# Layer 1's first chunk gets its keys and queries inside layer 0's last batch

## The chip, the cores and the metric

The kernel runs on one core of one Trainium2 chip. A core has a matrix engine (TensorE, "PE" in the profile, with its weight loads as "PEld"), a vector engine (VectorE, "DVE"), a scalar engine for activations (ScalarE, "ACT"), a general engine (GpSimd, "POOL") and an engine that here only issues DMA transfers (SyncE, "SP"). Each engine takes its own instructions strictly in order and waits at semaphores for the others. The metric is the device time of one execution in microseconds; the profile shows one execution in detail.

## The reference

The input is `x`, 4 batches of 32 images of 128x128 pixels. Two layers follow each other.

Layer 0 is a Fourier attention block. Cut to its steps:

```python
xn = inorm(x)                                   # one channel per image
k, q, v = fno(xn, K), fno(xn, Q), fno(xn, V)    # 32 heads; spectral weights + a skip factor
p = softmax(q k^T over the 32 images of a batch)
av = p v
a = inorm(fno(av, P) + x)
m = fno(inorm(a), m0, inner_norm=True, act=gelu)
m = fno(m, m1, inner_norm=True)
out0 = inorm(m) + a
```

Layer 1 reads `out0` as 4 sequences of 4096 rows of 128 channels (an image's columns are the rows of the sequence). It normalises the rows, attends with additive scores (`score = sum_a w2[a] tanh(f_i[a] + g_j[a] + b1[a])`, strictly causal, exponentiated and normalised), adds, normalises again, and applies a router with 8 experts of which the best two are mixed, with a residual.

## The kernel before

**Layer 0** (`layer0`) loops over four batches `b`. A batch's spectrum `xd` was written to DRAM in the batch before. The stages of a batch: attention weights (`attention_weights`: products `pa` and `pb` of spectra on DVE and POOL, L473 and L475, summed by PE into `sp`, then a softmax from `mx` on, L509); the value products (L702 to L732: `xb` loaded from `xd` by SP in pairs, copied to PSUM by ACT as `xw`, multiplied with the weights `gb` into `u` on DVE, L719, and POOL, L717, summed over heads by PE into `po`); the back transform (`py`, evacuated into `yf`); a first spectrum, gelu (L844 to L854), a second spectrum (`spectra(1, gl)`: PE's `pz` and `px`, ACT's `z` and squares, DVE's `spec` and `part`, POOL's sum of the two, L804); and the last inverse transform into `xr`, stored to `x1` in DRAM by SP in four pieces (L910). For b below 3 the first stages of the next batch are put between these. The weights of layer 0 (`mcw`, `energy`, `cross`) are prepared once, before the first batch, ahead of `attention_weights(0, front)` in the program.

**Layer 1** (`layer1`) works on chunks of 1024 rows, four to a sequence. For a chunk, `prepare` loads `xc`, normalises it into `kx` (`norm_pieces`: statistics, aggregates, `scale` with a power on POOL, `apply`), transposes it into `xt` (`transpose_half`, PE's `pt`) and makes keys and queries (`as_keys`, `as_queries`: PE's `pz`, ACT's exponential, SP's DMAs that exchange halves of partitions into `kf` and `qf`). Keys of a sequence, `ke` and `kf`, stay in SBUF for its four chunks. The attention itself runs over units of up to 512 queries by 128 keys: PE makes `d` and `n` (L1297), ACT takes a logarithm and an exponential (L1350, L1362), DVE multiplies (L1355), POOL adds (L1358, L1359), ACT takes an exponential (L1366), and PE sums with `kx` (L1316). `finish` does the router and the experts.

**Order.** Outside of the attention's loop a scheduler of the framework orders each engine's instructions by priority (program order) and readiness by its own estimates. The attention's loop is under `manual_schedule`: its order is written out, and the remaining steps of other chunks (`pieces`) are dealt out among the units with budgets for DVE and POOL. Chunk 1's transposes are the first such pieces and stand on PE directly behind the first unit's `d`. Memory comes from pools; a pool entered after another has been left takes over its memory and waits for what still uses it. Before, all pools of layer 1 open after all of layer 0's are closed, and chunks 0 and 1 are prepared at the head of layer 1:

```python
    norm, pieces = begin(0, beside=False)
    norm_1, todo = begin(1, beside=False)
    for piece in norm + pieces + norm_1:
        piece[-1]()
```

The router and expert weights (`wr`, `we`, L936 to L984) and the maps `mq`, `mk` for queries and keys (L989 to L1014) are made ahead of that, all through one PSUM buffer (`misc`).

Of the kernel before, what the change touches and what calls it, by code (L numbers as in the profile page):

```python
# [7 lines left out]
F32 = mybir.dt.float32  # L8
AF = mybir.ActivationFunctionType
ALU = mybir.AluOpType  # L10
AX = mybir.AxisListType
PSUM = bass.MemoryType.PSUM

P = 128
B, T, H, C = 4, 32, 128, 128
# [5 lines left out]
A = 16  # L21
GROUP_SIZES = (6, 5, 5)
DSCALE = 128.0
NE = 8
IC = 1024
NB = IC // P
# [5 lines left out]
B1, W2, RB = 11, 27, 43  # L32
NSMALL = 51
# [41 lines left out]
NM = KX * KY  # L75
# [29 lines left out]
def layer0(  # L105
    tc, x, kq_modes, kq_mirror, vcw, pcw, m0cw, m1cw, mcol0, heads, heads_row, small_row, by_p, inv_cols, dram, x1
):
    nc = tc.nc
    pools = [tc.tile_pool(name="l0_const", bufs=1), tc.tile_pool(name="l0_ps", bufs=2, space=PSUM)]
    pools.append(tc.tile_pool(name="l0_x", bufs=2))  # L110
    const, ps, images = (p.__enter__() for p in pools)
# [21 lines left out]
    def columns(n):  # L133
# [8 lines left out]
    par = const.tile([P, NSMALL], F32, name="par")  # L142
    nc.sync.dma_start(out=par, in_=small_row.partition_broadcast(P))
    ident = const.tile([P, P], F32, name="ident")
# [14 lines left out]
    gb = const.tile([P, 2, 2, NM], F32, name="gb")  # L159
# [7 lines left out]
        tc.tile_pool(name="l0_modes", bufs=1),  # L167
    ]
    grp, small, modes = (p.__enter__() for p in work)
# [409 lines left out]


# [44 lines left out]
    prep_pool.__exit__(None, None, None)  # L625
    work = [tc.tile_pool(name="l0_big", bufs=1), tc.tile_pool(name="l0_xb", bufs=4)]
    big, late = (p.__enter__() for p in work)
    pools += work
    weights = attention_weights(0, front)

    for b in range(B):
# [63 lines left out]
        for x0 in range(0, KX, NK):  # L695
# [36 lines left out]
            nc.scalar.copy(rs[:, x0 : x0 + nk].rearrange("p x y -> p (x y)"), po)  # L732
        yf = big.tile([P, T, 2, KY], F32, name=f"yf_{b}", tag="spec")
# [126 lines left out]
        if b + 1 < B:  # L860
            normed = image_sums(b + 1, loaded)

# [53 lines left out]
def layer1(tc, x1, w1t_in, signs, vec17, expert_w, expert_b, router_w, small_row, out):  # L916
    nc = tc.nc
    nblk = T
    pools = [
        tc.tile_pool(name="l1_const", bufs=1),  # L920
        tc.tile_pool(name="l1_keys", bufs=2),
        tc.tile_pool(name="l1_work", bufs=2),
        tc.tile_pool(name="l1_small", bufs=2),
        tc.tile_pool(name="l1_ps", bufs=1, space=PSUM),
    ]
    const, keys, work, small, ps = (p.__enter__() for p in pools)

    tc.keep_in_program_order(nc.scalar.preload_act_table_set("natural_log_exp_and_others"))
    ident = const.tile([P, P], F32, name="ident1")
    make_identity(nc, ident)  # L930
    par = const.tile([P, NSMALL], F32, name="par1")
    nc.sync.dma_start(out=par, in_=small_row.partition_broadcast(P))
    nhalf = const.tile([P, 1], F32, name="nhalf1")
    nc.vector.memset(nhalf, -0.5)
    wr = const.tile([P, NE], F32, name="wr")
    nc.sync.dma_start(out=wr, in_=router_w)  # L936
    we = const.tile([P, NE, C], F32, name="we")
    nc.scalar.dma_start(out=we, in_=expert_w.rearrange("e d c -> d e c"))

    later = const.tile([P, 2, P], F32, name="later")  # L940
    nc.gpsimd.memset(later, 1.0)
    nc.gpsimd.affine_select(
        out=later,
        in_=later,
        compare_op=ALU.is_gt,
        fill=0.0,
        base=0,
        pattern=[[0, 2], [1, P]],
        channel_multiplier=-1,
    )  # L950

    rank = const.tile([P, NE], F32, name="rank")
    for e in range(NE):
        nc.vector.memset(rank[:, e : e + 1], float(NE - e))

    centre = const.tile([P, P + 1], F32, name="centre")
    nc.vector.tensor_scalar(centre[:, :P], ident, 1.0 / C, None, ALU.subtract)
    nc.vector.memset(centre[:, P:], 1.0 / C)

    banks = ["m"]  # L960

    def misc(name):
        banks.append(banks.pop(0))
        return ps.tile([P, 512], F32, name=name, tag=banks[-1])

    mean = const.tile([P, P], F32, name="mean")
    nc.vector.memset(mean, 1.0 / C)
    eb = work.tile([P, NE, C], F32, name="eb", tag="xt", bufs=1)  # L970
    nc.scalar.dma_start(
        out=eb.rearrange("p e c -> p (e c)"),
        in_=expert_b.rearrange("e c -> (e c)").partition_broadcast(P),
    )
    for w, row in (
        (wr, par[:, RB : RB + NE]),
        (we[:, :4].rearrange("p e c -> p (e c)"), eb[:, :4].rearrange("p e c -> p (e c)")),
        (we[:, 4:].rearrange("p e c -> p (e c)"), eb[:, 4:].rearrange("p e c -> p (e c)")),
    ):
        n = w.shape[1]  # L980
        pm = misc("pm")[:, :n]
        nc.tensor.matmul(pm, mean, w, start=True, stop=True)
        nc.vector.tensor_tensor(w, w, pm, ALU.subtract)
        nc.vector.scalar_tensor_tensor(w, row, 1.0 / C, w, ALU.mult, ALU.add)  # L984

    sg = const.tile([A + 1, P], F32, name="sg")
    nc.sync.dma_start(out=sg, in_=signs)  # L989
    w1t = const.tile([A, 2, P], F32, name="w1t")  # L990
    nc.sync.dma_start(out=w1t, in_=w1t_in)
    v17 = const.tile([A + 1, 2], F32, name="v17")
    nc.sync.dma_start(out=v17, in_=vec17)
    mq, mk = (const.tile([P, P], F32, name=n) for n in ("mq", "mk"))
# [6 lines left out]
    sgv = const.tile([P, 2], F32, name="sgv")  # L1001
    nc.vector.tensor_copy(sgv, pv[:, :2])

    one = const.tile([P, 1], F32, name="one1")
# [4 lines left out]
    off = const.tile([P, 2], F32, name="off")  # L1009
# [3 lines left out]
    kmul = const.tile([P, 1], F32, name="kmul")  # L1013
# [10 lines left out]
    def norm_pieces(src, dst, nb, beside=True):  # L1024


        st = small.tile([P, NB, 6], F32, name="st", tag="ln_st", bufs=3)
        mv = small.tile([P, NB, 2], F32, name="mv", tag="ln_mv", bufs=3)
        r = small.tile([P, NB], F32, name="r", tag="ln_r", bufs=3)
        mr = small.tile([P, NB], F32, name="mr", tag="ln_mr", bufs=3)  # L1030
# [37 lines left out]
    def prepare(b, i0, own, beside):  # L1068
# [4 lines left out]
        xc = work.tile([P, NB, C], F32, name="xc", tag="xc", bufs=4)  # L1073
        nc.sync.dma_start(out=xc, in_=x1[b, i0 : i0 + NB].rearrange("t w c -> w t c"))
        own_kx = kx[:, i0 : i0 + NB]
        xt = work.tile([P, IC], F32, name="xt", tag="xt", bufs=1)
        qe, qf = (work.tile([P, IC], F32, name=n, tag=n, bufs=3) for n in ("qe", "qf"))

        def as_keys(h):
# [4 lines left out]
            ks = work.tile([P, 512], F32, name="ks", tag="ks", bufs=1)  # L1084
# [19 lines left out]
        return (qe, qf), load + sums + after, pieces  # L1104

# [113 lines left out]
    chunks = [(b, i0) for b in range(B) for i0 in range(0, nblk, NB)]  # L1219
# [10 lines left out]
    state = {}  # L1230
    sums = {}
    live = {}

    def begin(c, beside=True):
        b, i0 = chunks[c]
        if i0 == 0:

            own = (keys.tile([P, nblk, C], F32, name=f"kx_{b}", tag="kx"),) + tuple(
                keys.tile([P, nblk * P], F32, name=f"{n}_{b}", tag=n) for n in ("ke", "kf")
            )  # L1240
        else:
            own = state[c - 1][0]
        qs, norm, pieces = prepare(b, i0, own, beside)
        state[c] = (own, qs)
        return norm, pieces

# [88 lines left out]
    norm, pieces = begin(0, beside=False)  # L1335
    norm_1, todo = begin(1, beside=False)
    for piece in norm + pieces + norm_1:
        piece[-1]()
# [79 lines left out]
    for p in reversed(pools):  # L1418
        p.__exit__(None, None, None)
# [72 lines left out]
```

## Time and profile before

| | |
|---|---|
| median of 3 runs | 3216.72 us (3215.26 to 3219.33) |
| the profiled execution's own time | 3214.14 us |
| its span, first to last instruction | 3212.4 us |
| mean granted TensorE clock | 0.963 |
| busy, share of span | PE 92%, DVE 72%, ACT 72%, POOL 66% |
| layer 0 | up to about 1095 us |
| layer 1 | from there to the end |

A row of the profile's timelines has start and duration in us, then engine, source line, operation, output<-inputs by the program's names, and in brackets how long the engine had idled and what ended that. Rows of neighbouring instructions of one kind are merged (x8). The table of stretches has, for each stretch, its length, each engine's busy time with the number of instructions, the granted clock as a share of full speed, the mean share of the 16 DMA engines, and GB/s. The line numbers are those of the kernel before.

### The profile page before, as it was taken

To read this page: it belongs to the slowest core of one execution; us is meant where nothing else is said; L and a number is where in the kernel's file an instruction comes from. 1 tells how busy PE (TensorE), PEld (TensorE's weight loads), DVE (VectorE), ACT (ScalarE), POOL (GpSimd) and SP (SyncE) were. 2 spreads that over 40 slices of the span, in tenths; PEclk is the share of its full clock that TensorE was granted. 3 is DMA by queue.
4 is the path that set the end of the run, shared out by engine and by line. 5 is a ranking of instruction groups with operands and counts; after the bars stand their busy time and mean duration, and the time that the engine had idled before them with its cause. 6 is when DMAs were issued, how large, how long until landed. Compare 5 with 4: busy or idle time off the path is not lost.

```text
span 3212.4 us, 53393 instructions
## 1 busy us (share of the span) xinstructions
PE 2971.1 (92%) x19698; PEld 1558.3 (49%) x19698; DVE 2317.7 (72%) x5072; ACT 2323.7 (72%) x3205; POOL 2134.2 (66%) x1879
## 2 busy tenths in 40 slices
PE   7899899899898699999999999999999999999997
PEld 5378367458558544444344443444444434444443
DVE  5767767768777556777666868866777777687887
ACT  2344344354344389999999999998999999999992
POOL 1631641461460278878788897889878889888773
PEclk7899899999998799999999999999999999999998
DMA  6301310230130111010110000011100010101000
GB/s 137 102 25 24 100 50 3 63 108 1 39 107 1 55 45 30 7 31 8 30 37 24 14 24 14 8 32 30 29 24 14 14 37 24 37 1 31 14 14 14
DMA packets 151925, 112.57 MB, mean 35 GB/s; under 512 B 36750, under 2 KB 140273, under 8 KB 151057
## 3 DMA queue, kind: packets, MB, share of 16 engines
q1 hardware_dynamic: 135825, 103.40, 12.0%
q10 hardware_dynamic: 15840, 5.77, 0.8%
q8 instruction: 156, 2.56, 0.3%
q14 instruction: 104, 0.85, 0.1%
HBM read 68.16 MB, written 20.00 MB: 27 GB/s over the span
## 4 chain that ended last, share of the span: by engine, by line
PE 59%; POOL 11%; ACT 8%; DVE 7%; issue 5%; DMA 0%; POOLq 0%; DVEq 0%; ACTq 0%; SPq 0%
PE d L1297 19%; PE po L1316 11%; PE px L1185 6%; ACT r L1350 4%; PE n L1297 4%; PE po L722 3%; POOL e L1359 3%; POOL e L1358 3%; PE four L257 2%; PE pv L252 2%; PE px L243 2%; PE px L242 2%; POOL kx L1050 1%; ACT e L1366 1%; PE pz L233 1%
## 5 line engine op out<-in xcount | busy, mean ns | idle before, releaser
L1355 DVE TENSOR_TENSOR r<-n,r 128x1024 f32<-128x1024 f32 (+1 forms) x1056 | 962.1, 953 | 479.9 <-PE n L1297 392.5
L1358 POOL TENSOR_TENSOR e<-r 128x512 f32<-128x512 f32 x528 | 673.0, 1275 | 268.7 <-DVE r L1355 268.1
L1350 ACT ACTIVATE r<-d 128x1024 f32<-128x1024 f32 (+1 forms) x1056 | 792.9, 802 | 65.5 <-PE n L1297 58.8
L1362 ACT ACTIVATE r<-r 128x1536 f32<-128x1536 f32 x528 | 783.5, 1484 | 16.7
L1359 POOL TENSOR_TENSOR e<-e,r 128x512 f32<-128x512 f32 x528 | 671.2, 1271 | 41.4
L1297 PE MATMUL d<-qe,ke 32*128 32x512 f32 (+3 forms) x2304 | 610.0, 604 | 38.3 <-ACT r L1350 36.5
L1316 PE MATMUL po<-e,kx 128*128 128x512 f32 (+3 forms) x1152 | 594.7, 605 | 15.0 <-POOL e L1371 15.0
L1297 PE MATMUL n<-qe,ke 32*128 32x512 f32 (+3 forms) x2304 | 607.4, 603 | 0.0
L1297 PE MATMUL d<-qf,kf 32*128 32x512 f32 (+3 forms) x2304 | 554.8, 556 | 0.0
L1297 PE MATMUL n<-qf,kf 32*128 32x512 f32 (+3 forms) x2304 | 554.5, 556 | 0.0
L1189 DVE SCALAR_TENSOR_TENSOR xc<-px,wgt,xc 128x128 f32<-128x128 f32 x1024 | 358.3, 350 | 41.2 <-PE px L1185 10.4
L1366 ACT ACTIVATE e<-e 128x512 f32<-128x512 f32 x528 | 325.6, 617 | 65.1 <-POOL e L1359 64.3
L1316 PEld LDWEIGHTS po<-e,kx 128*128 128x128 f32 x1152 | 175.6, 188 | 393.5 <-issue 310.1
L1297 PEld LDWEIGHTS d<-qe,ke 32*128 32x128 f32 x2304 | 177.4, 184 | 359.7 <-ACT r L1350 340.3
L717 POOL TENSOR_TENSOR u<-xb,gb 128x858 f32<-128x858 f32 (+1 forms) x120 | 234.8, 1987 | 115.1 <-PE po L722 104.7
L1297 PEld LDWEIGHTS d<-qf,kf 32*128 32x128 f32 x2304 | 221.5, 187 | 177.1 <-issue 164.7
L804 POOL TENSOR_TENSOR spec<-spec,part 128x264 f32<-128x264 f32 x64 | 55.0, 860 | 377.2 <-DVE part L801 173.6
L1185 PE MATMUL px<-we,x2t 128*128 128x512 f32 x512 | 265.2, 603 | 6.9 <-DVE xc L1189 6.0
L719 DVE TENSOR_TENSOR u<-xw,gb 128x858 f32<-128x858 f32 (+1 forms) x200 | 206.5, 1083 | 48.5 <-PE po L722 32.4
L1297 PEld LDWEIGHTS n<-qf,kf 32*128 32x128 f32 x2304 | 228.9, 186 | 19.8 <-issue 12.5
L722 PE MATMUL po<-u,pr 128*32 128x429 f32 (+1 forms) x1280 | 187.7, 537 | 18.3 <-POOL u L717 8.7
L1297 PEld LDWEIGHTS n<-qe,ke 32*128 32x128 f32 x2304 | 177.8, 183 | 10.0 <-DVE r L1355 1.2
(353 smaller groups left out, 4185.9 us busy)
## 6 DMA issues: line engine op xcount, KB each, us to landing
xb<-xd SPq DMA_DIRECT2D x128, 214.5 KB
xc<-x SPq DMA_DIRECT2D x31, 512.0 KB
x<-x SPq DMA_DIRECT2D x16, 512.0 KB
qf<-qe SPq DMA_DIRECT2D x64, 128.0 KB
out<-xc SPq DMA_DIRECT2D x15, 512.0 KB
xb<-xd SPq DMA_DIRECT2D x32, 198.0 KB
gb<-gd SPq DMA_DIRECT2D x4, 1056.0 KB
x<-in_x SPq DMA_DIRECT2D x8, 512.0 KB
```

What stands on the lines that cost most here:

```text
L717: nc.gpsimd.tensor_tensor(u, xb, gk, ALU.mult)
L722: nc.tensor.matmul(po[32 * j : 32 * j + 32], pr[:, i, k], u[:, r], start=i == 0 and k == 0, stop=i == 3 and k == 1,)
L1185: nc.tensor.matmul(px, x2t[:, k * P : (k + 1) * P], we[:, e0 : e0 + 4], start=True, stop=True)
L1189: nc.vector.scalar_tensor_tensor(xc[:, k], px[:, e], wgt[:, k, e0 + e : e0 + e + 1], xc[:, k], ALU.mult, ALU.add)
L1297: nc.tensor.matmul(o, k, q, start=turn == 0 or g > 0, stop=turn == 1 or g > 0)
L1316: nc.tensor.matmul(sums[c, h][:, q0 : q0 + c1 - c0], kx[:, jb], e[:, c0:c1], start=jb == 0, stop=is_last and q0 > 2 * P, skip_group_check= ...
L1350: nc.scalar.activation(r[:, g], d, AF.Ln, scale=1.0 / DSCALE)
L1355: nc.vector.tensor_tensor(r[:, g], part, r[:, g], ALU.mult)
L1358: nc.gpsimd.tensor_tensor(e, r[:, 1], r[:, 2], ALU.add)
L1359: nc.gpsimd.tensor_tensor(e, e, r[:, 0], ALU.add)
L1362: nc.scalar.activation(r, r, AF.Exp, scale=-1.0)
L1366: nc.scalar.activation(e, e, AF.Exp)
```

## The change

Layer 1 becomes a generator that is run in two parts. Its first part, entered from layer 0's last batch just behind the gelu in program order, opens a pool `l1_first` and prepares chunk 0 up to its keys and queries. That pool lies in SBUF at the other side of the memory, where layer 0's value weights `gb`, its spectra `xx` and the `xb` buffers were; these three now have pools of their own at that side, and are left in the last batch as soon as its value products are done. Chunk 0's input, its transposes and the scaled keys `ks` go through `spare`, a buffer of layer 0's images, and its PSUM through layer 0's `wide` buffers. The second part is the rest of layer 1. The constants that chunk 0 needs (`ident`, `sg`, `w1t`, `mq`, `mk`, the biases) move with it. In layer 0 `attention_weights(0, front)` moves ahead of the preparation of `mcw`, `energy` and `cross`. The cores of the diff:

```diff
 def layer0(..., dram, x1, first):
+    right = [
+        tc.tile_pool(name="l0_gb", bufs=1, side="right"),
+        tc.tile_pool(name="l0_modes", bufs=1, side="right"),
+    ]
...
+    prep_pool.__exit__(None, None, None)
+    pools.append(tc.tile_pool(name="l0_big", bufs=1))
+    right.append(tc.tile_pool(name="l0_xb", bufs=4, side="right"))
+    big, late = (p.__enter__() for p in (pools[-1], right[-1]))
+    weights = attention_weights(0, front)
     mcw, energy, cross = [], [], []
...
-    prep_pool.__exit__(None, None, None)
-    work = [tc.tile_pool(name="l0_big", bufs=1), tc.tile_pool(name="l0_xb", bufs=4)]
-    big, late = (p.__enter__() for p in work)
-    pools += work
-    weights = attention_weights(0, front)
...
             nc.scalar.copy(rs[:, x0 : x0 + nk].rearrange("p x y -> p (x y)"), po)
+        if b + 1 == B:
+            for p in reversed(right):
+                p.__exit__(None, None, None)
...
         logarithms()
         if b + 1 < B:
             normed = image_sums(b + 1, loaded)
+        else:
+            first((ps, images))
...
 def layer1(tc, x1, ..., out):
+    before, images = yield
+    first_pool = tc.tile_pool(name="l1_first", bufs=1, side="right")
+    first = first_pool.__enter__()
+    spare = images.tile([P, T, C], F32, name="spare", tag="x")
...
     def misc(name):
+        if not pools:
+            return before.tile([P, 512], F32, name=name, tag="wide")
...
+        if pools:
+            xc = work.tile([P, NB, C], F32, name="xc", tag="xc", bufs=4)
+            xt = work.tile([P, IC], F32, name="xt", tag="xt", bufs=1)
+        else:
+            xc, xt = spare[:, :NB], spare[:, NB : 2 * NB].rearrange("p k c -> p (k c)")
...
+    norm, pieces = begin(0, beside=False)
+    for piece in norm + pieces:
+        piece[-1]()
+    yield
+    pools += [ ... the pools of the rest of layer 1 ... ]
...
-    norm, pieces = begin(0, beside=False)
     norm_1, todo = begin(1, beside=False)
-    for piece in norm + pieces + norm_1:
+    for piece in norm_1:
         piece[-1]()
...
+        second = layer1(tc, x1, ..., out)
+        next(second)
         layer0(tc, ..., dram, x1, second.send)
+        for _ in second:
+            pass
```

Keys of the sequences 0 and 2 and queries of every third chunk live in `l1_first`, the others in the later pools, so that as many buffers rotate as before.

## The prediction

> **What bounds the kernel now.** I read the page first (busy shares and the chain of waits), then the table of stretches to find where layer 0 ends and layer 1 begins, then the timelines of those places.
>
> ```profile
> PE 59%; POOL 11%; ACT 8%; DVE 7%; issue 5%; DMA 0%; POOLq 0%; DVEq 0%; ACTq 0%; SPq 0%
> ```
>
> TensorE carries most of the chain, so work that is added to PE in a full stage costs its whole length, and a stage in which PE waits is where time can be won. The table of stretches (PE, PEld, DVE, ACT, POOL busy; granted clock; DMA share; GB/s):
>
> ```profile
> 1032.00:1041.00 9.00, 9.00 (x50) 9.00 (x50) 5.52 (x21) 4.26 (x10) 0.00 (x0) 0.58 0.01 2
> 1041.00:1063.00 22.00, 20.88 (x179) 20.17 (x177) 10.81 (x35) 9.03 (x22) 5.19 (x7) 1.00 0.00 1
> ...
> 1094.00:1126.00 32.00, 15.68 (x30) 6.81 (x30) 16.55 (x85) 1.37 (x2) 5.84 (x7) 0.50 0.38 107
> 1126.00:1134.00 8.00, 8.00 (x11) 2.17 (x10) 0.00 (x0) 2.40 (x3) 1.56 (x1) 0.50 0.42 96
> ```
>
> From 1094.9 us (the last result of layer 0) to about 1135 PE only prepares layer 1, half idle and at half clock. 1032 to 1063 is the last batch's second spectrum, where PE is full. The timeline of the passage:
>
> ```profile
> 1099.61 0.57 PE L982 MATMUL pm<-wr,mean 128*128 128x8 f32 x2 [5.84 <-DMA wr<-in_router_w]
> ...
> 1106.20 0.79 PE L997 MATMUL pm<-sg,w1t 16*128 16x128 f32 x2 [0.78 <-DVE we L983]
> ...
> 1119.51 1.65 POOL L1044 TENSOR_TENSOR r<-r,nhalf 128x8 f32<-128x8 f32 x1 [5.91 <-DVE r L1043]
> ...
> 1121.60 2.69 DVE L1050 TENSOR_SCALAR kx<-xc,r,mr 128x128 f32<-128x128 f32 x8
> ...
> 1132.73 1.02 ACT L1350 ACTIVATE r<-d 128x1024 f32<-128x1024 f32 x1 [1.35 <-PE d L1297]
> ...
> 1134.29 1.11 PE L1065 MATMUL pt<-ident,kx 128*128 128x128 f32 x4
> ```
>
> Line by line: PE's first step waits for the router weights until 1099.6; then come the expert weights, then the key and query maps and chunk 0's keys and queries; the power at 1119.5 and the `kx` at 1121.6 are chunk 1's norm; the attention's first logarithm is at 1132.7; chunk 1's transposes, which the hand-written order puts behind the first unit, end at 1135.4. From there the rows are attention proper. A second place is batch 0's attention weights, on DVE:
>
> ```profile
> 82.23 0.29 DVE L591 COPY mcw<-mcw_raw 128x66 f32<-128x66 f32 x1 [2.54 <-DMA mcw_raw<-in_m1cw]
> 82.44 1.21 DVE L473 TENSOR_TENSOR pb<-xp,xm 128x1024 f32<-128x1024 f32 x1
> 83.58 0.85 DVE L594 TENSOR_TENSOR msq<-mcw 128x66 f32<-128x66 f32 x1
> ...
> 89.52 1.21 DVE L473 TENSOR_TENSOR pb<-xp,xm 128x1024 f32<-128x1024 f32 x1
> ```
>
> DVE stands 2.54 us for the weights of the last convolution in the middle of its products `pa`, `pb`.
>
> **The change, part by part.** The order of each engine's instructions in the changed kernel can be read before it runs; the durations are those of the profiled execution (3214.14 us, of which 3212.4 are span).
>
> *A, weights of layer 0 later.* All of `mcw1`'s DVE work now stands after the last `pa` and before `mx`. From 79.7 (end of the `pa` before) to 89.52 DVE did four products (4 x 1.14 = 4.6 us) in 9.8 us: 5.2 us were the wait and the small operations. After 89.52 products follow without a gap to 102.05, so DVE sets the end there; POOL's `pb` (two of 1.9 us per three of DVE's groups of 4.5 us) and PE have room. The small operations, 2.6 us, now lie where DVE idled 5.28 us before `mx` (102.05 to 107.33), and their DMAs were issued by 82.2. The value products' first `xb` was issued at 83.4 and the DMA share has fallen to 0.23 from 96 on, so the value products can follow earlier. Gain 5.2; if the `xb` loads behind image 1's took half of it back, 2.6.
>
> *B, chunk 0's load.* It is put on SP's queue behind the last store of batch 2 and ahead of fifteen of the last batch's twenty pairs of `xb` loads. It overwrites the buffer which those stores read, so SP stands until the last has landed:
>
> ```profile
> 891.88 3.10 DMA x<-x
> ```
> ```profile
> 895.41 1.22 SPq L702 DMA_DIRECT2D xb<-xd  x2
> ```
>
> The first is of the chain of waits, the second of SP's timeline: landed at 894.98, next `xb` at 895.41 anyway. The wait costs 0.4 us. Behind it are the `xb` loads, ACT's copies `xw` and all of `u`. The load itself: a store of the same 512 KB moved at 291 GB/s in the DMA row, 1.8 us. The Trainium skill (DMA: Bandwidth & Descriptors, "Queues, rings and completion order") says that one queue's descriptors are consumed in ring order on each engine; so the `xb` start behind all of it: 2.2 us late by the rule. In the trace the DMA engines are only about half busy there (share 0.49 from 885 to 900), and the next use of `xb`, at 899.17, waited for DVE and not for DMA; the one at 903.32 waited 1.1 us for DMA while PE went on. I take 1.2, between 0 (a gain is excluded, as nothing is taken off the queue) and 3.7 (two late pairs).
>
> *C, chunk 0's norm, 955 to 968.* On DVE 8 statistics (1.7), 8 aggregates (0.6), scale with POOL's power (1.65) and one `kx`: from 957.7, when POOL's last `u` frees the memory, to 962.8. DVE was idle 6.98 us up to 963.28, its next evacuation of `yf`. So it is free, with 0.5 us to spare; the other seven `kx` (0.26 each) lie between evacuations 4 us apart. If the cover failed it would cost what it overruns, PE's `py` standing behind it. SP's three small loads and POOL's `ident` fall into idle time.
>
> *D, keys and queries of chunk 0, 1023 to 1053.* The two `pm` fall into the gelu stretch, in which PE idled 4.6 us: free. The rest goes to PE where it was full. `pv` and two `pc`: 1.4 us at half clock (the rows at 1108 to 1110). Eight transposes: two halves of 1.1 at half clock, 1.1 together at full. Four `pz`: 1.12 each at full clock (the rows of chunk 1), 2.08 at half. Then waits: two PSUM buffers for four `pz`, so the third `pz` waits for ACT's first exponential, the fourth for the second; and ACT now takes `z` only after its table load. Laid out by hand from the last gelu (1043.0): table 1.28, `z` 0.6, `ke` 0.69, DVE's `z` to 1046.0, `z` 0.38, `qe` 0.69, last `pz` to 1048.2, then the remaining 3.4 us of `px`: 1051.7 where it was 1044.7. Cost 7.3 (I allow 0.3 for late `ks` on POOL, 1.6 each, ahead of the `spec` sums). PE's work alone is 1.4 + 1.1 + 4.5 = 7.0; the ends are 5.5 (the chain's wait for ACT and DVE at 1051, 1.5 us, swallows a part) and 10.8 (all `pz` at half clock). The ten 128 KB DMAs that this issues on SP go when no other DMA runs and 30 us before the stores queued behind them.
>
> *E, the passage.* Gone: 1106.2 to 1132. Now PE issues two `d`, then `pm<-wr` (still 1099.6, for the router weights), `d`, `pm`, `d`, `pm`: at half clock, 2.07 each, to 1108.4. DVE does chunk 1's statistics between, the second `we` at 1108.5 to 1110, aggregates to 1111.8, POOL's power to 1113.7, four `kx` to 1115.2. PE stands there: chunk 1's transposes are next in its order. They end at 1116.3 where they ended at 1135.4: 19.1 us earlier. What is late next is chunk 1's norm, not chunk 0's keys. But PE has idled 7 us before it. The second unit's products (1135.4 to 1139.1) lose nothing by that, as they ran cold before too; the third's (2.2 us) ran at full clock:
>
> ```profile
> 1134.00:1136.00 2.00, 2.00 (x11) 1.31 (x14) 0.56 (x1) 1.57 (x2) 0.00 (x0) 0.50 0.47 108
> 1136.00:1139.00 3.00, 3.00 (x25) 2.12 (x18) 0.13 (x1) 0.51 (x1) 0.00 (x0) 0.57 0.00 0
> ```
>
> The Trainium skill's rule (TensorE: Matmul & The Clock Gate, "Part 1: The HAM clock gate") is that the clock is half by default and doubles after one busy window of about 3.4 us: then it is full by the third unit, 5 us after 1115.2, and nothing is lost. In this trace PE was full from 1031.6, after an idle of 4.6 us, and stayed at 0.50 until 1039.6, 8 us; by that the third unit runs cold and ends 2.0 us later. I take the trace: gain 19.1 - 2.0 = 17.1, by the rule 19.1. Bounds: 20.9 (clock full for the second unit already) and 14.4 (the fourth unit cold too, 2.7 more beyond ACT's pace of 4.1 us a unit). Behind it ACT's chain sets the pace as before.
>
> Sum: -5.2 + 1.2 + 0 + 7.3 - 17.1 = -13.8, to 3200.3 for the profiled execution. The median of the runs is 2.6 above that execution, so the forecast is 3216.7 - 13.8 = 3202.9. Ends: -5.2 - 20.9 + 5.5 = -20.6, and -2.6 - 14.4 + 10.8 + 3.7 = -2.5.
>
> **Rivals.** About 0.2%, 6.4 us, is what a measurement of this kernel can tell from no change.
>
> 1. The wait only moves. If chunk 1's norm does not come earlier (its first four `kx` ended at 1122.9), its transposes end at 1124, the gain in E is 11.4, or 9.4 with a cold third unit, and the sum is -6.1: 3210.6, at the edge of no change. For it: chunk 1's statistics share DVE with the `we` updates. Against it: its load no longer stands behind chunk 0's, and DVE loses half its work there.
>
> 2. Slower: the clock. The second spectrum runs at 1.00 with PE busy 20.88 us. If the waits in D drop the clock at 1043 and it stays down, that is up to 20.9 us more: sum +7.1, 3223.8. It decides from 13.8 of those 20.9 on. For it: an idle of 4.6 us before 1031.6 cost 8 us at 0.50. Against it: the waits in D are of 1 us.
>
> 3. More is won: PE warm at the second unit, D at its lower end, nothing lost in B: -20.6, 3196.1.
>
> That the change doesn't do what it says is excluded by the order: chunk 0's matmuls do stand in the last batch.
>
> **How the numbers follow.** My forecast 0.71, rival 1 0.15, rival 2 0.05, rival 3 0.09. The range 3196 to 3214 holds the forecast's ends and rival 1. Faster: 0.67 of the forecast, 0.06 of rival 1, 0.09: 0.82. Same: 0.04 and 0.09: 0.13. Slower: 0.05.
>
> **What would show it.** A: no wait at `mcw`, `mx` near 102. B: `xw` waits for DMA near 900. C: the `yf` evacuation where it was. D: from `py` to the last store 7 us longer, with `pz` waiting for ACT `ke` and `qe`. E: from the last `x` of layer 0 to the first long logarithm 26 us less, to chunk 1's transposes 19. I am wrong if D exceeds 12, if the clock at the second spectrum is not 1.00, or if the attention proper gets longer.

## The result, and the profile after

The changed kernel takes 3203.94 us (median of 4 runs, 3198.89 to 3207.05), beside 3215.99 us of the kernel before on the same chip (4 runs): a ratio of 0.996, 95% interval 0.9943 to 0.9978, or 12.05 us less. A second group of runs of the same changed kernel (after_again below) gave 10.8 us less. The profiled execution took 3203.55 us, of which 3201.8 are span, at a mean granted clock of 0.966. The chain of waits:

```profile
PE 55%; POOL 13%; ACT 9%; DVE 7%; issue 6%; DMA 1%; POOLq 0%; DVEq 0%; ACTq 0%; SPq 0%
```

TensorE still carries it. The table of stretches of the changed kernel (PE, PEld, DVE, ACT, POOL busy; granted clock; DMA share; GB/s) for the last batch and the passage:

```profile
1027.00:1036.00 9.00, 8.98 (x40) 8.64 (x41) 4.58 (x20) 4.07 (x10) 0.00 (x0) 0.50 0.01 2
1036.00:1044.00 8.00, 8.00 (x34) 5.71 (x34) 5.05 (x20) 5.82 (x10) 1.70 (x2) 0.78 0.07 16
1044.00:1066.00 22.00, 20.85 (x177) 20.15 (x176) 8.62 (x23) 6.53 (x17) 6.73 (x8) 1.00 0.24 55
1066.00:1078.00 12.00, 9.64 (x50) 9.67 (x51) 7.42 (x18) 1.53 (x4) 1.68 (x1) 0.57 0.01 1
...
1101.00:1124.00 23.00, 12.39 (x22) 4.27 (x26) 8.89 (x48) 3.10 (x3) 2.08 (x2) 0.50 0.35 107
```

PE is full from 1036 to 1044, where chunk 0's keys and queries were put in. The second spectrum (1044 to 1066) runs at full clock, as before, so the clock did not fall over the waits. The stretch behind it, the last inverse transform, is now at 0.57. The passage into layer 1 (1101 to 1124) is still half idle and at half clock, but shorter. PE's timeline of the passage:

```profile
1101.88 2.08 PE L1336 MATMUL d<-qe,ke 32*128 32x512 f32 x4 [1.31 <-DVE x L914]
...
1107.85 0.57 PE L1159 MATMUL pm<-wr,mean 128*128 128x8 f32 x2 [3.90 <-DMA wr<-in_router_w]
...
1114.35 2.08 PE L1159 MATMUL pm<-we,mean 128*128 128x512 f32 x2
...
1122.27 1.24 PE L1029 MATMUL pt<-ident,kx 128*128 128x128 f32 x4 [5.84 <-DVE kx L1014]
```

and ACT's:

```profile
1110.45 1.02 ACT L1388 ACTIVATE r<-d 128x1024 f32<-128x1024 f32 x1 [11.63 <-PE d L1336]
```

Attention products `d` now stand directly behind the last result of layer 0. Chunk 1's transposes wait 5.84 us for its norm: that is what is late next, as foreseen.

To compare stages between runs, each is measured between two events of its own profile (one profile for each kernel, us). *Value stage*: from the issue of the DMA `prd<-ph`, at the end of batch 3's attention weights, to the end of the first spectrum's `px`. *Gelu and second spectrum*: from the first `pv` behind that to the last `px`. *Last inverse*: to the end of the last `four`. *Passage*: to chunk 1's transposes. *Attention*: to the end of the span.

| kernel | value stage | gelu and second spectrum | last inverse | passage | attention |
|---|---|---|---|---|---|
| before | 129.24 | 51.82 | 31.52 | 40.52 | 2078.11 |
| before_with_a | 130.52 | 48.19 | 33.23 | 42.04 | 2079.24 |
| after | 130.45 | 56.84 | 35.40 | 21.71 | 2079.53 |
| after_again | 127.50 | 59.56 | 37.63 | 22.03 | 2079.63 |
| after_without_a | 130.32 | 58.35 | 34.40 | 21.43 | 2079.04 |
| keys_gap | 128.78 | 60.76 | 32.92 | 21.31 | 2079.47 |
| keys_gap2 | 131.64 | 53.49 | 31.17 | 21.73 | 2078.31 |
| norm1 | 128.83 | 66.80 | 43.62 | 16.25 | 2076.61 |
| norm1_lw | 128.87 | 62.82 | 43.62 | 5.03 | 2079.00 |
| gap2_lw | 131.74 | 56.32 | 31.13 | 17.13 | 2079.19 |
| all2 | 134.69 | 49.73 | 44.17 | 5.02 | 2079.25 |
| all5 | 137.37 | 49.48 | 31.50 | 5.02 | 2079.61 |
| all4 | 132.37 | 51.90 | 31.56 | 5.03 | 2079.70 |
| spt_on_dve | 130.19 | 56.85 | 35.42 | 22.23 | 2076.70 |

What lies ahead of these stages differs by up to 17 us between single profiles (the value stage begins between 867 and 884 us), although past batch 0's weights the order is the same in all of them. So the spans of single executions are not compared; stages and medians are. Each ratio below is to the kernel before, run beside the kernel on the same chip; three chips were used, so kernels of different groups are compared by their ratios.

### The profile page after: what moved, and what is told of

The parts are those of the page before. It is cut to its first block, busy times and chain, and to the rows that moved or that the text cites. A ratio compares the mean times of both kernels' runs of the same rounds, so it can differ in the third digit from the quotient of the medians.

```text
span 3201.8 us, 53401 instructions
## 1 busy us (share of the span) xinstructions
PE 2961.4 (92%) x19698; PEld 1554.2 (49%) x19698; DVE 2316.0 (72%) x5072; ACT 2324.2 (73%) x3205; POOL 2135.2 (67%) x1879
## 4 chain that ended last, share of the span: by engine, by line
PE 55%; POOL 13%; ACT 9%; DVE 7%; issue 6%; DMA 1%; POOLq 0%; DVEq 0%; ACTq 0%; SPq 0%
PE d L1336 18%; PE po L1355 10%; PE px L1242 5%; ACT r L1388 5%; POOL e L1396 3%; POOL e L1397 3%; PE n L1336 3%; PE po L726 3%; PE four L261 2%; PE pv L256 2%; PE px L247 2%; PE px L246 2%; ACT e L1404 2%; POOL kx L1014 2%; DVE r L1393 2%
## 5 line engine op out<-in xcount | busy, mean ns | idle before, releaser
L1336 PE MATMUL d<-qe,ke 32*128 32x512 f32 (+3 forms) x2304 | 605.7, 602 | 39.5 <-ACT r L1388 36.1
L723 DVE TENSOR_TENSOR u<-xw,gb 128x858 f32<-128x858 f32 (+1 forms) x200 | 206.7, 1086 | 51.3 <-PE po L726 34.4
```

Source lines behind the costliest of these rows:

```text
L1336: nc.tensor.matmul(o, k, q, start=turn == 0 or g > 0, stop=turn == 1 or g > 0)
```

## The experiments

**Part A alone, and all but part A.** In before_with_a the kernel before gets only the earlier attention weights; in after_without_a the changed kernel loses only those.

```diff
--- before_with_a (the kernel before)
+    prep_pool.__exit__(None, None, None)
+    ...
+    weights = attention_weights(0, front)
     mcw, energy, cross = [], [], []
...
-    weights = attention_weights(0, front)
--- after_without_a (the changed kernel)
-    weights = attention_weights(0, front)
     mcw, energy, cross = [], [], []
...
+    weights = attention_weights(0, front)
```

> The kernel before with step A alone: batch 0's attention weights moved ahead of the preparation of mcw, energy and cross. The forecast's step says -5.2 us against before in every execution. The theory after seeing the changed kernel's trace: the products end 5.2 us earlier, but ACT's spt stands behind two xw copies that wait for the xb loads (landed near 90.7 us), so A pays about 5 us where PE's clock was at half from 44 to 60 us (mx near 102), and about 0 where it was at full speed there (mx near 97.4, the products done by 88). Timed against before: between -5.2 and 0. Rival: A is worth nothing at all (within 1 us).

Measured: 3211.83 us (7 runs), 6.5 less than before; ratio 0.9974 (0.9964 to 0.9985).

> The changed kernel with step A undone: the preparation of mcw, energy and cross again ahead of batch 0's attention weights. By the forecast 5.2 us slower than the changed kernel, that is 6.9 to 8.6 us faster than before. By the theory of the gate (xw waiting for xb ahead of spt) 0 to 5 us slower than the changed kernel, so 7 to 12 us faster than before. The passage from layer 0 to layer 1 is the same as in the changed kernel under both.

> The changed kernel once more, as the measure for the other three and for what its profile does by chance. Theory: the half or full clock from 44 to 60 us (half in the profile of before, full in that of the changed kernel, with the same instructions in the same order) is chance and may fall either way here; the passage (chunk 1's first transpose about 20 us after the last result of layer 0) and the second spectrum (7.5 us longer than before from the last gelu's inverse to the last px) come out the same within 1 us. Rival: the clock there follows from the change, so it is full again, and would be half in every kernel without A.

Measured: after_without_a 3210.80 us (7 runs), ratio 0.9973 (0.9962 to 0.9984); after_again, the changed kernel itself beside it, 3207.59 us (6 runs), ratio 0.9962 (0.9949 to 0.9975). The difference, 3.2 us, is less than the 6.5, but the two intervals overlap. The trace is sharper, with one profile of each. From the first score `sc` to `mx` before took 36.06 us, before_with_a 30.6 and after_again 30.7, at a similar granted clock from 44 to 60 us, where the products are made (0.50, 0.50, 0.61): 5.4 less. In after_without_a that clock was 0.93, and its DVE shows what is then lost:

```profile
80.78 0.20 DVE L599 COPY mcw<-mcw_raw 128x66 f32<-128x66 f32 x1 [11.52 <-DMA mcw_raw<-in_m1cw]
...
105.14 0.68 DVE L513 TENSOR_REDUCE mx<-sc 64x16 f32<-64x512 f32 x1 [5.27 <-PE sc L502]
```

In the two profiles with this order DVE has the weights of the last convolution at 80.8 us (clock 0.93) and at 82.2 (0.50), nearly the same time; a PE that was quicker until then only makes DVE wait longer for them, 11.52 us here and 2.54 before. `mx` comes 44.3 us after the first score, and in four profiles with part A at the same clock 34.7 to 36.1. So A is worth 5.4 at half clock and 8 to 10 near full clock, by single profiles. Which clock the products get is not set by the change: the changed kernel had 0.93 in one profile and 0.61 in the other, with the same instructions.

**The copy in front of the scores.** At full clock the changed kernel's `mx` waits for something else. Its ACT:

```profile
90.73 0.52 ACT L715 COPY xw<-xb 128x429 f32<-128x429 f32 x1 [0.32 <-DMA xb<-xd]
91.18 0.58 ACT L491 COPY spt<-sp 128x512 f32<-128x512 f32 x1
```

The copy of the summed products, `spt`, stands behind value-product copies that wait for a DMA. In spt_on_dve batch 0's copy is moved to DVE:

```diff
-        nc.scalar.copy(spt, sp)
+        (nc.vector.tensor_copy if b == 0 else nc.scalar.copy)(spt, sp)
```

> The changed kernel with batch 0's copy spt on DVE instead of ACT, where it stood behind two xw copies that wait for the loads xb (one look; it tells something only if the clock from 44 to 60 us is full again). Theory: in such an execution the step from the first sc to mx took 34.7 to 36.1 us though the products were done after 26; without the gate it takes 31 to 34. Where the clock is half there, 30.7 as in the changed kernel. Rival: 36 as before, because mx waits for something else.

Measured, in a single run: 3203.11 us. From `sc` to `mx` 35.1 us at a clock of 0.61, where after_again needed 30.7 at 0.61: it lost 4.4. On DVE the copy stands behind the small operations on `mcw`, and PE, idle until then, made the scores at a lower clock (1.72 us, 1.04 in after_again):

```profile
98.67 1.72 PE L502 MATMUL sc<-spt,cst 128*32 128x512 f32 x2 [2.69 <-DVE spt L491]
```

The wait was moved to another queue. The clock for which the copy was moved did not come in this run, so what the move would give there is not shown.

**Chunk 0's four `pz` out of the spectrum.** In keys_gap the maps and transposes stay behind the gelu, and keys and queries come behind the second spectrum, where PE waits for `spec`.

```diff
--- layer1: the products of keys and queries
+            if not pools:
+                tc.keep_in_program_order(i_k)
...
     norm, pieces = begin(0, beside=False)
-    for piece in norm + pieces:
+    for piece in norm + pieces[:2]:
+        piece[-1]()
+    yield
+    for piece in pieces[2:]:
         piece[-1]()
     yield
--- layer0, behind spectra(1, gl)
+        else:
+            first(None)
```

> The changed kernel with the four products pz of chunk 0's keys and queries pinned behind the last px of the second spectrum, where PE waited 3.2 us for spec, instead of in front of it. Theory: step D costs 7.5 us because it stands where PE is full; in the wait four products (4.1 us with ACT's exponentials between) cost about 1 us, and PE stays warm for the pv products behind it, which ran at half clock in the changed kernel and cost 4 us there: 4.5 to 8 us faster than the changed kernel, last px 4.5 to 5 us earlier against the first px. Rival: the wait only moves, as ms and v stand behind the exponentials on ACT and in PSUM: within 2 us of the changed kernel.

Measured: 3201.64 us (6 runs), ratio 0.9947 (0.9932 to 0.9962), 6 us less than after_again, with overlapping intervals. The gelu and second spectrum got no shorter (60.8 us, 56.8 to 59.6 in the changed kernel), though the products (4.5 us at full clock) were gone from it. What got shorter is the last inverse, 32.9 instead of 34.4 to 37.6. In the changed kernel PE was full where the products stood, so there they were paid for; taken away, they left a wait in their place. The order on ACT shows where it comes from. Before:

```profile
1039.55 0.38 ACT L178 ACTIVATE z<-pz 128x256 f32<-128x256 f32 x1 [0.63 <-DVE z L180]
1041.07 0.60 ACT L178 ACTIVATE z<-pz 128x512 f32<-128x512 f32 x1 [1.13 <-PE pz L233]
1041.56 1.63 ACT L847 ACTIVATE g<-g,hb,hs 128x128 f32<-128x128 f32 x4
1043.21 1.28 ACT L121 ACT_TABLE_LOAD   x1
```

The first evacuations `z` were ahead of gelu's last calls and of the table load, and PE started on `px` with them at 1040.87, 2.3 us ahead of the load. After:

```profile
1039.32 1.28 ACT L126 ACT_TABLE_LOAD   x1
1040.61 0.60 ACT L182 ACTIVATE z<-pz 128x512 f32<-128x512 f32 x1
1041.28 0.69 ACT L1055 ACTIVATE ke<-pz,off 128x512 f32<-128x512 f32 x1
```

and in keys_gap:

```profile
1032.64 1.28 ACT L126 ACT_TABLE_LOAD   x1
1033.93 0.60 ACT L182 ACTIVATE z<-pz 128x512 f32<-128x512 f32 x1
```

In both, ACT's `z` comes behind the table load, and the first `px` 3.7 and 2.5 us after the load's start. In keys_gap DVE's share of `z`, which stands behind the copies of chunk 0's transposes, then comes at 1034.39, and PE waits for it:

```profile
1035.13 1.02 PE L246 MATMUL px<-cst,z 128*128 128x99 f32 x4 [1.90 <-DVE z L184]
```

The clock hides a part of the gain. Behind this wait keys_gap's PE, full, ran at half clock, where the changed kernel's `px` ran at 1.00:

```profile
1035.30:1042.10 6.80, 6.80 (x33) 6.80 (x34) 1.65 (x7) 0.47 (x2) 0.74 (x1) 0.50 0.00 0
```

That is an estimated 3.4 us (half of 6.8). Without it the stage would be 57.4 us, 0.9 below the changed kernel's mean of 58.25: still far from the 4.5 of the products.

**Maps and transposes ahead of the first spectrum.** keys_gap2 is keys_gap with chunk 0's first pieces entered ahead of the first spectrum instead of behind the gelu, so that the second spectrum's own order is left alone.

```diff
+        if b + 1 == B:
+            first((ps, images))
         spec, sq = spectra(0, q)
...
-        else:
-            first((ps, images))
```

> As keys_gap, but chunk 0's norm, maps and transposes stand in front of the first spectrum, so that nothing of chunk 0 is left between gelu and the second spectrum. In keys_gap the second spectrum got no shorter (39.5 us from the fourth four to the last px, 38.1 in the changed kernel, 30.7 before): PE waited there for z, which ACT takes only after gelu's last call and its table load, and DVE after the two copies of the transposes. Theory: step D's cost is that order, not PE's work: with the order of before again the second spectrum takes 30 to 32 us, the four pz lie in the wait behind it, the first spectrum takes 1 to 2 us more, and the kernel is 4 to 7 us faster than the changed one and 2 to 4 faster than keys_gap. Rival: it is PE's work that counts, which is then paid in the first spectrum and in the last inverse: within 2 us of the changed kernel.

Measured: 3195.14 us (6 runs), ratio 0.9933 (0.992 to 0.9946), against 0.9962 of the changed kernel. The second spectrum's stage is 53.5 us (before: 51.8 and 48.2), the last inverse 31.2. ACT takes its first `z` ahead of the table load again:

```profile
1034.89 0.60 ACT L182 ACTIVATE z<-pz 128x512 f32<-128x512 f32 x1 [0.24 <-PE pz L237]
...
1036.65 1.28 ACT L126 ACT_TABLE_LOAD   x1
```

Its second `z` is still behind the load, and the clock again fell to 0.50 for 6.8 us, from 1038.3 on; gap2_lw below, with the same order here, took 56.3 us. In all2, all5 and all4 below both `z` are ahead of the load, as before, the clock at the spectrum is 1.00, and the stage takes 49.5 to 51.9 us, as before. In all4:

```profile
1048.03 0.60 ACT L182 ACTIVATE z<-pz 128x512 f32<-128x512 f32 x1 [1.15 <-PE pz L237]
...
1050.18 1.28 ACT L126 ACT_TABLE_LOAD   x1
```

So chunk 0's work had been put into the one place where it pushed the spectrum's first evacuations behind gelu's end. One thing is not separated: against keys_gap, keys_gap2 also takes the maps' and transposes' own time on PE, some 3 us, out of this stage. It isn't free ahead of the first spectrum either: the value stage, which holds that, is 131.6 to 137.4 us in the five kernels of this order, and 127.5 to 130.5 in the others. Of the step from keys_gap to keys_gap2 alone the intervals overlap; it is the two together that are faster than the changed kernel (their interval ends below that of after_again and just meets that of the first runs, 0.9943 to 0.9978).

**Chunk 1's norm earlier.** norm1 loads chunk 1 into `spare` and takes its norm into the last batch, with its statistics held behind the last products of the inverse transform; norm1_lw also puts the centring of router and expert weights (the `pm`) among the attention's pieces.

```diff
--- norm1: layer1, behind the first yield; layer0, ahead of the last inverse
+    xc_1 = spare[:, NB : 2 * NB]
+    nc.sync.dma_start(out=xc_1, in_=x1[0, NB : 2 * NB].rearrange("t w c -> w t c"))
+    for piece in sum(norm_pieces(xc_1, ..., NB, False), []):
+        piece[-1]()
+    yield
--- norm1_lw: in addition
-    for w, row in ( ... ):
+    weights = ( ... )
+    def centred(w, row):
...
+    todo[2:2] = [(SOME, 0.4 if k == 0 else 1.4, 0.0, lambda k=k: centred(*weights[k])) for k in range(3)]
```

> The changed kernel with chunk 1's load and norm also in layer 0's last batch (its input in spare, its eight statistics pinned on DVE behind the last cq, where DVE waits 5.7 us for x). The forecast's step E says that chunk 1's norm is what is late next: in the changed kernel PE waits 5.84 us for kx in front of chunk 1's transposes. Theory: that wait goes, the transposes start about 15 us after the first d instead of 20.5, and the kernel is 5 to 6 us faster than the changed one. Rivals: the wait only moves to the we products and their DMA (gain under 2 us); or DVE's 5 us in the last inverse put x off by as much (gain 0).

> As norm1, and the centring of the router and expert weights (wr, we) taken out of the passage and dealt out behind chunk 1's transposes among the attention's units. Theory: nothing is then between the first unit's four d and chunk 1's transposes: they start 8 to 9 us after the first d (20.5 in the changed kernel), 10 to 12 us faster than the changed kernel, less up to 2 us that the three pieces cost on DVE in later units. Rival: ACT's chain of logarithms and exponentials sets the pace already from the first d on, so no more than norm1's gain is to be had (within 2 us of it).

Measured: norm1 3210.61 us (17 runs), ratio 0.9974 (0.9965 to 0.9984); norm1_lw 3201.59 us (6 runs), ratio 0.9944 (0.9929 to 0.996). In norm1 the wait for `kx` in the passage is gone (16.25 us instead of about 21.7), and in norm1_lw the passage is 5.03 us: the transposes come 3.7 us after the first `d`. But the last inverse grew by about 8 us, to 43.6. DVE's timeline in norm1:

```profile
1088.79 2.31 DVE L1013 TENSOR_TENSOR ln_mr<-ln_mv,ln_r 128x8 f32<-128x8 f32 x1 [1.84 <-POOL ln_r L1012]
1091.13 2.27 DVE L1014 TENSOR_SCALAR ln_mr<-ln_mr 128x8 f32<-128x8 f32 x1
1093.44 6.19 DVE L1018 TENSOR_SCALAR kx<-spare,ln_r,ln_mr 128x128 f32<-128x128 f32 x8
```

The eight `kx` took 6.19 us together, where 2.13 is usual, and two operations on 128x8 elements 2.3 each. Beside them POOL adds up `x`; these are its rows, and one of the `kx` alone:

```profile
1088.73 4.65 POOL L911 TENSOR_TENSOR x<-x,g 128x1024 f32<-128x1024 f32 x2
1094.10 2.40 POOL L911 TENSOR_TENSOR x<-x,g 128x1024 f32<-128x1024 f32 x1 [0.72 <-ACT g L904]
1097.18 2.38 POOL L911 TENSOR_TENSOR x<-x,g 128x1024 f32<-128x1024 f32 x1 [0.67 <-ACT g L904]
```
```profile
1094.22 2.37 DVE L1018 TENSOR_SCALAR kx<-spare,ln_r,ln_mr 128x128 f32<-128x128 f32 x1
```

Six of the eight took 0.33 to 0.34 us. The fourth and the eighth, begun while a sum of POOL ran, lasted until it was over, and so did the two small operations: each of these four ends within 0.1 us of the end of a sum. DVE's last sums `x` stand behind the slow norm, and PE's last `four` behind those. The second spectrum's stage was longer too (66.8 and 62.8). About 3 us of that are again 6.8 us at half clock; the rest was not separated.

**Weights alone, and everything together.** gap2_lw is keys_gap2 with the centring among the pieces. all2 is keys_gap2 with both edits of norm1_lw. all5 is all2 with chunk 1's norm where POOL has little to do: its input goes into a free quarter of `spare`, and the norm stands ahead of the first spectrum with chunk 0's; its statistics are held in their place in the program. all4 is all5 without holding them.

```diff
--- all5
+        if b + 1 == B:
+            first((ps, images))
         spec, sq = spectra(0, q)
...
+    for piece in norm + pieces[:2]:
+        piece[-1]()
+    xc_1 = spare[:, 3 * NB : 4 * NB]
+    nc.sync.dma_start(out=xc_1, in_=x1[0, NB : 2 * NB].rearrange("t w c -> w t c"))
+    for piece in sum(norm_pieces(xc_1, ..., NB, False), []):
+        piece[-1]()
+    yield
+    for piece in pieces[2:]:
+        piece[-1]()
--- all4
-                if state and not pools and "xc_1" in held:
-                    tc.keep_in_program_order(i)
```

> keys_gap2 with the router and expert weights dealt out into the attention, chunk 1's norm left in the passage. Theory: PE waits for chunk 1's kx, which follows its load (issued behind the last store, landed 10 to 11 us after the last result): transposes 15 to 17 us after the last four instead of 21.7, 4 to 6 us faster than keys_gap2. Rival: the load of chunk 1 lands as late as before and kx with it: within 2 us of keys_gap2.

Measured: 3196.67 us (5 runs), ratio 0.9926 (0.9914 to 0.9939), not to be told from keys_gap2: the passage fell to 17.1 us, since chunk 1's norm is still late.

> All together: keys_gap2's places for chunk 0, norm1's for chunk 1 and the weights dealt out as in norm1_lw. If the three gains are independent, 14 to 19 us faster than the changed kernel (25 to 30 faster than before). Rival: they overlap, since each ends at ACT's pace in the attention: no more than the best single one, 10 to 12 us faster than the changed kernel.

Measured: 3192.84 us (6 runs), ratio 0.9923 (0.9909 to 0.9938). The passage is 5.0 us, but the last inverse is 44.2: the gain is handed back as in norm1.

> As all2, but chunk 1's input goes to a part of spare that is free from the start, and its norm stands at the head of the first spectrum, where POOL is idle. In norm1, norm1_lw and all2 DVE's kx of chunk 1 ran beside POOL's sums x of the last inverse and took 0.77 us each instead of 0.27, two small operations 2.3 us each instead of 0.17, and the inverse took 43.6 to 44.2 us from the last px to the last four instead of 31 to 37. Theory: with POOL idle the operations take 0.27 and 0.17 again, the last inverse 31 to 33, the passage stays at 5.0 us from the last four to the transposes, and the first spectrum takes up to 4 us more: 6 to 10 us faster than all2 (3183 to 3187 at all2's level of 3192.8). Rival: it was not POOL but the length of the chain itself, so the same 9 us are lost in the first spectrum: within 2 us of all2.

> As all5, with chunk 1's statistics not pinned: they stand beside chunk 0's in front of the evacuation of yf, where DVE had 0.5 us to spare beside chunk 0's norm. By step C of the forecast what the cover does not hide is paid in full: the evacuation 2 to 4 us later, the first spectrum not lengthened; within 2 us of all5. Rival: POOL's last u and DVE collide there too, 5 us or more slower than all5.

Measured: all5 3184.19 us (5 runs), ratio 0.9898 (0.9884 to 0.9912); all4 3179.80 us (4 runs), ratio 0.9884 (0.987 to 0.9897), the best kernel here, 39.9 us less than before and well ahead of the changed kernel. The last inverse is 31.5 and 31.6. Chunk 1's `kx` in all5:

```profile
998.54 2.13 DVE L1018 TENSOR_SCALAR kx<-spare,ln_r,ln_mr 128x128 f32<-128x128 f32 x8
```

That is 0.33 to 0.34 us each, one begun every 0.26: the same instruction, with no sum of POOL beside it. PE's passage in all4:

```profile
1089.81 5.49 PE L261 MATMUL four<-icol,v 66*128 66x128 f32 x24 [7.54 <-DVE x L916]
...
1102.08 2.08 PE L1354 MATMUL d<-qe,ke 32*128 32x512 f32 x4 [1.31 <-DVE x L916]
...
1105.80 1.12 PE L1031 MATMUL pt<-ident,kx 128*128 128x128 f32 x4
```

Chunk 1's transposes follow the first unit's products with no wait in front of them. Whether all4 is faster than all5 is not shown, as the intervals overlap.

## Why the prediction was right, step by step

The direction and the total held: 12.05 and 10.8 us less, where 13.8 were forecast. The steps held less evenly.

- **A, -5.2.** Right in place and size at half clock: -5.4 in the trace, -6.5 in the time of A alone (interval 0.9964 to 0.9985). The `mx` was named near 102; it came at 101.7 in before_with_a. What the forecast did not see is that A grows with the clock, to 8 to 10, as the late DMA landed at nearly the same time in both.
- **B, +1.2, and C, 0.** Nothing shows: the value stage takes 127.5 to 130.5 us in the three kernels with the changed tail and 129.2 to 130.5 in the two with the tail of before. The sign named for B, `xw` waiting for DMA near 900, is missing. SP's timeline of the changed kernel:

```profile
891.88 0.36 SPq L1042 DMA_DIRECT2D spare<-x  x1
892.34 3.70 SPq L706 DMA_DIRECT2D xb<-xd  x4
```

The first `xb` was issued 17.67 us after `prd<-ph`, 17.42 before. That is 0.25 us later at the issue, by one profile each (after_again has 16.1). The 2.2 that the forecast worked out from the rule of the Trainium skill (DMA: Bandwidth & Descriptors, "Queues, rings and completion order") would have had to show as copies that wait for DMA, and none does. B alone was not tried.

- **D, +7.3.** Seen +8.2: 58.25 as the mean of three kernels, 50.0 of two (which differ by 3.6 between themselves); from the fourth group of gelu's inverse to the last `px` it is 30.1 against 38.1. The hand layout in the forecast, with `z` behind the table load, was the right reading of the order; its waits of `pz` for ACT don't show, PE having no idle time from 1036 to 1044. The sentence beside it, that PE's work alone comes to 7.0, fits too, as PE was full there, but it is not what decides: keys_gap took 4.5 us of that work out and the stage stayed, even with the 3.4 us of its half clock set aside nearly so; it came back to its old length where both `z` were ahead of the table load again.
- **The last inverse, not in the forecast.** It is 3.4 us longer (35.8 as the mean of three, 32.4 of two). PE's `pv`, of before and then of the changed kernel:

```profile
1065.44 1.50 PE L252 MATMUL pv<-cst,spec 128*66 128x128 f32 x12 [3.20 <-DVE spec L808]
```
```profile
1068.36 2.80 PE L256 MATMUL pv<-cst,spec 128*66 128x128 f32 x12 [3.20 <-DVE spec L815]
```

The same 3.20 us of waiting, but then the half clock. It lasted 10.2 us in after and after_again and 3.4 in after_without_a; before_with_a, whose tail is that of before, had 3.4 us of it too (33.2), and before none (31.5). In keys_gap and keys_gap2, where `pz` fill that wait, the stage is 32.9 and 31.2. That the stage is longer by a lapse of the clock is shown by the rows; why the wait sets it off in one profile and not in another stays open, and with it how much of the 3.4 belongs to the change and how much to chance. The forecast ended its account of the last batch at the last `px`; this is the term it lacks.

- **E, -17.1.** Seen -19.6 up to chunk 1's transposes (21.7 against 41.3), forecast 19.1. Counted from the last `four` they were forecast within 0.3 us of where they came. The first long logarithm comes 9.9 us after that, 39.0 before: 29 earlier, forecast 26. Chunk 1's norm is late next, as was said. The cold third unit, +2.0 in the forecast and 0 by the rule of the Trainium skill (TensorE: Matmul & The Clock Gate, "Part 1: The HAM clock gate"), did not come: in the changed kernel the clock is 1.00 from 1128.2 on, 5.9 us after the transposes began, and the third unit's products start just behind that, as they do in after_again and after_without_a:

```profile
1124.80:1128.20 3.40, 3.40 (x22) 2.09 (x16) 0.86 (x1) 0.81 (x1) 0.00 (x0) 0.50 0.00 0
1128.20:1131.60 3.40, 3.22 (x35) 2.19 (x34) 2.44 (x4) 3.29 (x5) 2.55 (x2) 1.00 0.00 0
```
```profile
1128.46 0.59 PE L1336 MATMUL d<-qe,ke 32*128 32x384 f32 x2 [0.18 <-ACT r L1388]
```

Here the rule was right, and the 8 us that the forecast had taken from another stage were not. The attention stage's mean is 0.7 longer (2079.4 against 2078.7), but spt_on_dve, with the same order there, has 2076.7, so that is within what single profiles differ by. Net -18.9 with it.

The sum of the measured steps, with A at half clock, is -5.4 + 0 + 8.2 + 3.4 - 18.9 = -12.7. E gave 1.8 more than forecast, B cost 1.2 less and A gave 0.2 more; D cost 0.9 more, and the last inverse 3.4. That is the way from -13.8 to -12.7: errors of -3.2 and +4.3 nearly cancel, so that the total came out so close is in part luck. Rival 1, in which the wait only moves, is refuted by E; rival 2, a clock that stays down, did not come in the changed kernel's spectrum (it did, for 6.8 us, in that of keys_gap and keys_gap2), but a smaller form of it came one stage later.

## What to carry to other kernels

When work is moved into a full stage, look first at where it stands in each in-order queue, not at how long it takes: instructions of another stage that pushed the first evacuations behind a table load cost 8 us here, and one stage earlier only a part of that (2.2 us in keys_gap2: 131.6 in the value stage against a mean of 129.4 in the kernels that have nothing there). What is gained by moving a chain forward ends at the next chain that was hidden behind it (here chunk 1's norm, then the weights), so move these along, and to a place where they don't run beside long instructions of another engine that hold them up (here POOL's sums). All of it together won 39.9 us, where the first step alone won 11 to 12.

## What the runs showed of the hardware

**DVE beside POOL.** In norm1 a `kx`, a scale and offset of 128x128 elements, took 2.37 us when it began while POOL added up `x`, and 0.34 when it did not; on 128x8 elements the norm's two small operations took 2.31 and 2.27 us instead of 0.17. All four ended with one of POOL's sums (2.35 to 2.40 us long): DVE was not slowed, it stood until POOL was through. The Trainium skill (GPSIMD Engine Reference, "1. Specifications") says that POOL shares its SBUF interfaces with DVE and contends with some of its instructions; this case shows its size. In norm1 these ten instructions took 10.8 us instead of 2.5, so the standing alone was worth 8.3 us. The whole step from all2 to all5, 12.7 us in the last inverse (44.2 to 31.5, one profile each), also holds the norm's own work and a clock of 0.71 against 0.84. No run took POOL's sums away and left the norm in place; that POOL is the cause is read from the ends of the instructions.

**A clock that stays down while PE is full.** In all profiles the granted clock changed only at whole multiples of 3.413 us from one another, to within 0.03 us, with a phase that differs from run to run (before: at 29.27, 77.06, 83.89, 90.71 and 111.19 us, that is 14, 2, 2 and 6 steps). This agrees with the Trainium skill (TensorE: Matmul & The Clock Gate, "Part 1: The HAM clock gate"), which gives a window of 3.413 us that runs freely. But the section also has the clock full after one busy window. In the passage that was so (E above); in batch 0 it was not. Batch 0 of the kernel before, first over one step of its grid, then of both kernels over the same 4 us:

```profile
49.75:53.16 3.41, 3.41 (x18) 3.41 (x17) 0.68 (x3) 0.00 (x0) 0.00 (x0) 0.50 0.49 118
```
```profile
48.00:52.00 4.00, 4.00 (x20) 4.00 (x21) 0.68 (x3) 0.00 (x0) 0.00 (x0) 0.50 0.63 131
```
```profile
48.00:52.00 4.00, 4.00 (x39) 4.00 (x37) 1.99 (x8) 1.26 (x3) 0.00 (x0) 1.00 0.62 127
```

In the kernel before PE and its weight loads were busy without a gap over five whole steps of the grid, 49.75 to 66.82 us, within a stretch of 47.8 us at 0.50; the same products ran at 1.00 in the other profile. What the profiles do differ in is the grid's place. Counted from the first instruction, it has an edge at 45.07 to 46.18 us in the five profiles whose clock from 44 to 60 us was 0.93, at 44.03 to 44.49 in the five with 0.61, and at 46.34 to 47.20 in the four with 0.50: three groups that don't overlap, sorted after the fact, and why the place matters is not shown. So the clock of this stage could not have been forecast from how busy PE is, and a cost worked out from it, such as A's, has to be given for both clocks.
